# A routed feed-forward kernel: one product for the places of a tile's tokens, and transposes of gathered tokens on VectorE

## The chip, the core and the metric

The kernel runs on one core of one Trainium2 chip. The metric is device time in microseconds, from runs of the compiled program; less is better. All times below are in microseconds (us) unless marked ns. The engines are named as in the profile: PE is TensorE's matmul, PEld its weight load, DVE is VectorE, ACT is ScalarE, POOL is GpSimd, and SP is the queue that issues most DMAs.

## The reference

Tokens `x` are 64 sequences of 32, each of width 256 (2048 tokens). Three residual steps follow each other: cross-attention of 16 heads to a context of 257 rows of 128, self-attention of 4 heads with a rotary embedding, and a feed-forward layer with 8 experts, of which each token takes two. Cut to the part that the change touches:

```python
def _L0_ffn_ref(x, Wr, br, Wl1, bl1, Wl2, bl2, biases_N):
    D, H, N, K = (256, 512, 8, 2)
    scores_BSN = jnp.einsum('bsd,nd->bsn', x, Wr) + br
    w_BSN = jax.nn.softmax(scores_BSN, axis=-1)
    _, idx_BSK = jax.lax.top_k(scores_BSN + biases_N[None, None, :], K)
    val_BSK = jnp.take_along_axis(w_BSN, idx_BSK, axis=-1)
    val_BSK = val_BSK / jnp.sum(val_BSK, axis=-1, keepdims=True)
...
    h_NM2H = jnp.einsum('md,ndh->nmh', x_MD, Wl1) + bl1[:, None, :]
    a_NMH, b_NMH = (h_NM2H[..., :H], h_NM2H[..., H:])
    y_NMD = jnp.einsum('nmh,nhd->nmd', jax.nn.silu(a_NMH) * b_NMH, Wl2) + bl2[:, None, :]
...
    y_MD = jnp.einsum('mn,nmd->md', ew_MN, y_NMD)
...
x = x + _L0_ffn_ref(_layernorm(x, axis=-1), ...)
```

## The kernel before

Everything is float32. The work is cut into 16 tiles of 128 tokens (four sequences each), and has two stages with an overlap between them.

**The attention stage.** A loop over 64 sequences (L971) writes out PE's order by hand. For each sequence it transposes the probabilities (`probs_transposed`, L336), issues the scores of the next sequence (L313) and mixes the context (L346). Between these steps, `step()` advances three generators: "near" and "far", which are `rest` (L532) of the two tiles before, and "ahead", the next queries. `rest(t)` does the output of cross-attention, self-attention and the routing of tile t. PE and SP keep the order of the code (L79); the order on DVE, ACT and POOL is chosen by the compiler's scheduler from the same program.

**Routing** (`route`, L474) has three parts between two yields. It transposes the normalised tokens `xr`. It forms the scores, the two best experts, `two` (one row of 8 for each choice, 0 or 1), `both` (their sum) and the weights of the experts, which are put into the row beside the token (a row `RW` is 256 numbers, 8 weights and the token's number). Then it finds each token's place among those of its expert: PE adds two products into `pk`, `before` × `both` (tokens of this tile that come earlier, L514) and `ones` × `seen` (all of the tiles before, L515). `at` adds the start of the expert's region, `seen` takes in `both` (L518), and `slots` are the two row numbers in the DRAM buffer `routed`, to which POOL scatters the tile's rows with two indirect DMAs (L525).

**The experts.** The rows of an expert are worked on in blocks of 128. Six early blocks are chosen from the counts after tile 12 (`early_blocks`), while the last tiles are still under way; up to 33 late ones are planned after tile 15 (`late_blocks`), of which 28 run in this trace. `counted` (L547) broadcasts the counts by the product of `ones` and `seen`. A block goes through these steps:
- `gathered` (L612): SP reads the block's first row from a small table and issues one DMA of 128 rows of 1060 B from `routed` into `xg` (five buffers).
- `weights` (L618): SP loads the expert's weights, 1028 KB and 640 KB, into one of three lanes, only if the expert differs from that of the block before in the lane.
- `prepared` (L628): PE transposes the two halves of the tokens into PSUM (L633), ACT copies them to `bxT` (L635, two buffers), DVE forms the block's gate and target rows (L638 to L647).
- `first_half` and `second_half` (L649, L666): 16 products (L661) of 128x128x128 into `pa` and `pb`, then ACT's silu (L675) and DVE's `g` (L680).
- `combined` (L687): four products (L692) of 256 columns, DVE's bias and gate (L697, L698) into `y` (four buffers), and POOL's indirect DMA that adds the 128 rows of `y` to the output (L699).

`run` (L1077) sets the order of PE and SP for the late blocks: in block b, the gather of b + 3, `prepared(b + 1)`, `first_half(b)`, `combined(b - 1)` and a weight load of b + 2, `second_half(b)`, and the other weight load of b + 3. In the first late block `last_early` (L1107) stands in the place of `combined`; it finishes the last early block and issues both weight loads of late block 2, behind the gather of block 3.

The parts that the change touches, with the profile's line numbers:

Of the kernel before, what the change touches and what calls it, by code (L numbers as in the profile page):

```python
# [16 lines left out]
P = 128  # L17
# [33 lines left out]
def block_kernel(  # L51
# [422 lines left out]
    def route(t, xr):  # L474

        nc.gpsimd.tensor_copy(xr[:, RW - 1 : RW], token[:, t : t + 1])
        xT = wk.tile([P, 2, P], FP, tag="xrT", name=f"xrT{t}")
        transposed(xT, xr, 2, f"r{t}", t < NT - 2)
        yield
        pr = bank([NE], f"pr{t}")  # L480
        for k in range(2):
            nc.tensor.matmul(pr, xT[:, k, :], wr_sb[:, k, :], start=(k == 0), stop=(k == 1))
        sc = sm.tile([P, NE], FP, tag="rsc", name=f"rsc{t}")
        nc.vector.tensor_tensor(sc, pr, br_bc, ALU.add)
        sel = sm.tile([P, NE], FP, tag="rsel", name=f"rsel{t}")
        nc.vector.tensor_tensor(sel, sc, bn_bc, ALU.add)
        top = sm.tile([P, 8], FP, tag="rtop", name=f"rtop{t}")
        nc.vector.max(top, sel)
        idx = sm.tile([P, 8], U32, tag="ridx", name=f"ridx{t}")
        nc.vector.max_index(idx, top, sel)  # L490
        idf = sm.tile([P, 2, 1], FP, tag="ridf", name=f"ridf{t}")
        nc.vector.tensor_copy(idf[:, :, 0], idx[:, 0:2])

        two = sm.tile([P, 2, NE], FP, tag="rtwo", name=f"rtwo{t}")
        nc.vector.tensor_tensor(
            two, expert_id2, idf.to_broadcast([P, 2, NE]), ALU.is_equal
        )
        both = sm.tile([P, NE], FP, tag="rboth", name=f"rboth{t}")
        nc.vector.tensor_tensor(both, two[:, 0, :], two[:, 1, :], ALU.add)
        nmx = sm.tile([P, 1], FP, tag="rnmx", name=f"rnmx{t}")  # L500
        nc.vector.tensor_reduce(nmx, sc, AX.X, ALU.max, negate=True)
        ex = sm.tile([P, NE], FP, tag="rex", name=f"rex{t}")
        nc.scalar.activation(ex, sc, AF.Exp, bias=nmx)
        nc.vector.tensor_tensor(ex, ex, both, ALU.mult)
        tot = sm.tile([P, 1], FP, tag="rtot", name=f"rtot{t}")
        nc.vector.tensor_reduce(tot, ex, AX.X, ALU.add)
        inv = sm.tile([P, 1], FP, tag="rinv", name=f"rinv{t}")
        nc.vector.reciprocal(inv, tot)
        ew = xr[:, D : D + NE]
        nc.vector.tensor_scalar(ew, ex, inv, None, ALU.mult)  # L510
        yield

        pk = bank([NE], f"pk{t}")
        nc.tensor.matmul(pk, before, both, start=True, stop=False)  # L514
        nc.tensor.matmul(pk, ones, seen, start=False, stop=True)  # L515
        at = sm.tile([P, 1, NE], FP, tag="rat", name=f"rat{t}")
        nc.vector.tensor_tensor(at[:, 0, :], pk, region[:, 0, :], ALU.add)
        nc.vector.tensor_tensor(seen, seen, both, ALU.add)  # L518
        nc.vector.tensor_tensor(two, two, at.to_broadcast([P, 2, NE]), ALU.mult)
        slot = sm.tile([P, 2], FP, tag="rslot", name=f"rslot{t}")  # L520
        nc.vector.tensor_reduce(slot, two, AX.X, ALU.add)
        slots = sm.tile([P, 2], U32, tag="rslots", name=f"rslots{t}")
        nc.vector.tensor_copy(slots, slot)
        for k in range(2):
            nc.gpsimd.indirect_dma_start(  # L525
                out=routed[:, :],
                out_offset=bass.IndirectOffsetOnAxis(ap=slots[:, k : k + 1], axis=0),
                in_=xr,
                in_offset=None,
            )  # L530

    def rest(t, cT, lastT, ut):  # L532

# [10 lines left out]
    def small(shape, name, dt=FP):  # L544
        return tb.tile([P] + shape, dt, name=name)

    def counted(name):  # L547

        pc = bank([NE], f"pc_{name}")
        nc.tensor.matmul(pc, ones, seen, start=True, stop=True)  # L550
        count = small([1, NE], f"count_{name}")
        nc.vector.tensor_copy(count[:, 0, :], pc)
        return count
# [35 lines left out]
    def number(meta, k, b, most):  # L589
        return nc.values_load(  # L590
            meta[0:1, k, b : b + 1],
            engines=[SP],
            min_val=0,
            max_val=most,
            skip_runtime_bounds_check_because="formed from counts that bound it",
        )

    class Blocks:
# [1 line left out]

        def __init__(self, name, n, lane):
            self.name, self.n, self.lane = name, n, lane
            self.meta = small([3, n], f"meta_{name}", U32)
            self.mine = small([n, NE], f"mine_{name}")
            self.gate = small([n], f"gate_{name}")
            self.to = small([n], f"to_{name}", U32)
            self.valid = self.spare = None
            self.xgs, self.xTs, self.ps, self.gs, self.experts = {}, {}, {}, {}, {}  # L610

        def gathered(self, b):  # L612
            xg = xp.tile([P, RW], FP, tag="xg", bufs=5, name=f"xg_{self.name}{b}")
            at = number(self.meta, 0, b, NE * CAP - P)
            nc.sync.dma_start(out=xg, in_=routed[bass.ds(at, P), :])
            self.xgs[b] = xg

        def weights(self, b, layers, sure=False):  # L618
            if b not in self.experts:
# [7 lines left out]

        def prepared(self, b):  # L628

            xg = self.xgs.pop(b)  # L630
            pt = bank([2, P], f"pxT_{self.name}{b}")
            for k in range(2):
                nc.tensor.transpose(pt[:, k, :], xg[:, k * P : (k + 1) * P], ident)  # L633
            xT = xp.tile([P, 2, P], FP, tag="bxT", bufs=2, name=f"bxT_{self.name}{b}")
            nc.scalar.copy(xT, pt)  # L635
            self.xTs[b] = xT
            gates = xp.tile([P, NE], FP, tag="gates", name=f"gates_{self.name}{b}")
            nc.vector.tensor_tensor(gates, xg[:, D : D + NE], self.mine[:, b, :], ALU.mult)  # L638
            one = slice(b, b + 1)
            nc.vector.tensor_reduce(self.gate[:, one], gates, AX.X, ALU.add)  # L640
            if self.valid is None:
                nc.vector.tensor_copy(self.to[:, one], xg[:, RW - 1 : RW])
            else:
                nc.vector.scalar_tensor_tensor(
                    self.to[:, one], xg[:, RW - 1 : RW], self.valid[:, one],
                    self.spare[:, one], ALU.mult, ALU.add,
                )  # L647

# [7 lines left out]
        def of_half(self, b, half):  # L656
            w, _ = lanes[self.lane(b)]
            for j in range(4):
                for k in range(2):
                    lo = k * 2 * HID + (half * 4 + j) * P  # L660
                    nc.tensor.matmul(  # L661
                        self.ps[b][half][:, j, :], w[:, lo : lo + P], self.xTs[b][:, k, :],
                        start=(k == 0), stop=(k == 1),
                    )

# [41 lines left out]
    def early_blocks():  # L707


        bl = Blocks("early", EARLY, lambda b: b % 2)  # L710
        count = counted("early")
        full = in_blocks(count, 0, "early")
        last = up_to(full, "early")
        wide = [P, EARLY, NE]
# [20 lines left out]

    def late_blocks(done):

        bl = Blocks("late", LATE, lambda b: (b + 2) % LANES)
        count = counted("late")
        nb = in_blocks(count, P - 1, "late")  # L740
        nc.vector.tensor_tensor(nb, nb, done, ALU.subtract)

# [180 lines left out]

    before = iota([P], [[1, P]], 0, -1, "before")
    nc.vector.tensor_scalar(before, before, 0.0, None, ALU.is_gt)
    region = iota([1, NE], [[0, 1], [CAP, NE]], 0, 0, "region")
    expert_id2 = iota([2, NE], [[0, 2], [1, NE]], 0, 0, "expert_id2")

# [6 lines left out]

    early = iota([EARLY // 2, 2], [[1, EARLY // 2], [EARLY // 2, 2]], 0, 0, "early")
    early_expert = iota([EARLY, NE], [[0, EARLY], [1, NE]], 0, 0, "early_expert")
    row = iota([1], [[0, 1]], 0, 1, "row")
    minus_spare = iota([1], [[0, 1]], -TOK, -1, "minus_spare")
    token = iota([NT], [[P, NT]], 0, 1, "token")  # L940

    seen = const.tile([P, NE], FP, name="seen")
    nc.gpsimd.memset(seen, 0.0)
    none = xp.tile([P, RW], FP, tag="xg", bufs=5, name="none")
    nc.gpsimd.memset(none, 0.0)

# [129 lines left out]

    def run(lo, hi, before=None):  # L1077
        for b in range(lo, hi):
            if b + 3 < hi:
                blocks.gathered(b + 3)  # L1080
            if b + 1 < hi:
                blocks.prepared(b + 1)
            blocks.first_half(b)
            if b > lo:
                blocks.combined(b - 1)
                if b - 1 + LANES < hi:
                    blocks.weights(b - 1 + LANES, (1,))
            elif before:
                before()
            blocks.second_half(b)  # L1090
            if b + LANES < hi:
                blocks.weights(b + LANES, (0,))
            if b == 4:
                yield
        blocks.combined(hi - 1)
# [83 lines left out]
```

## Time and profile before

| what | value |
|---|---|
| median of 3 runs | 806.24 us (805.84 to 806.75) |
| the profiled execution's own time | 805.53 us |
| its span, first to last instruction | 803.8 us |
| PE busy | 774.1 us, 96% |
| DVE busy | 495.8 us, 62% |
| ACT busy | 377.9 us, 47% |
| POOL busy | 143.6 us, 18% |
| mean granted clock of TensorE | 0.995 |
| L633 pxT_late on PE | 56 matmuls, mean 275 ns |
| L635 bxT_late on ACT | 28 copies, mean 372 ns |
| L514 and L515 on PE | 32 and 32 matmuls, median 216 and 256 ns |
| L699 out_x<-y_late on POOL | 28 indirect DMAs, mean 1554 ns |

Matmuls are pipelined, and the profile gives each one the time until its result is there; the time that one takes from the next is the distance of their starts. The page's slices cut the span into 40 stretches of 20.1 us, each digit a busy share in tenths. In the timeline a row reads: start, duration, engine, line, operation, output<-inputs, shapes, count, and in brackets the engine's idle time before it and what ended it. A row with "x4" merges four instructions. Releasers are inferred from semaphores, and a wait for several of them is put down to the one that came last by the profile.

### The profile page before, as it was taken

To read this page: it belongs to the slowest core of one execution; us is meant where nothing else is said; L and a number is where in the kernel's file an instruction comes from. 1 tells how busy PE (TensorE), PEld (TensorE's weight loads), DVE (VectorE), ACT (ScalarE), POOL (GpSimd) and SP (SyncE) were. 2 spreads that over 40 slices of the span, in tenths; PEclk is the share of its full clock that TensorE was granted. 3 is DMA by queue.
4 is the path that set the end of the run, shared out by engine and by line. 5 is a ranking of instruction groups with operands and counts; after the bars stand their busy time and mean duration, and the time that the engine had idled before them with its cause. 6 is when DMAs were issued, how large, how long until landed. Compare 5 with 4: busy or idle time off the path is not lost. (4 is left out here: it accounts for less than half of the span.)

```text
span 803.8 us, 15150 instructions
## 1 busy us (share of the span) xinstructions
PE 774.1 (96%) x5212; PEld 609.9 (76%) x5212; DVE 495.8 (62%) x2045; ACT 377.9 (47%) x1078; POOL 143.6 (18%) x195
## 2 busy tenths in 40 slices
PE   8899999999999999999999999999998999999994
PEld 6576777777767777776777777766688899999994
DVE  5567666766775676668676667767655734334332
ACT  3565555556455555546455545654426322232230
POOL 3001011120211111020111111021133313332332
PEclk9999999999999999999999999999999999999998
DMA  9520202121020102012020202110531594356321
GB/s 308 165 89 1 66 11 67 28 73 60 18 80 12 67 10 87 12 69 73 18 67 11 67 11 67 40 47 15 192 136 34 138 400 124 54 150 207 54 42 22
DMA packets 32735, 64.14 MB, mean 80 GB/s; under 512 B 5328, under 2 KB 23632, under 8 KB 31120
## 3 DMA queue, kind: packets, MB, share of 16 engines
q1 hardware_dynamic: 26128, 54.08, 19.9%
q0 software_dynamic: 6528, 9.06, 6.2%
q8 instruction: 43, 0.70, 0.3%
q14 instruction: 36, 0.29, 0.1%
HBM read 87.54 MB, written 13.16 MB: 125 GB/s over the span
## 5 line engine op out<-in xcount | busy, mean ns | idle before, releaser
L318 ACT ACTIVATE pr<-s,nmx 128x257 f32<-128x257 f32 x256 | 121.7, 479 | 108.6 <-DVE nmx L317 100.4
L317 DVE TENSOR_REDUCE nmx<-s 128x1 f32<-128x257 f32 x256 | 105.9, 421 | 71.2 <-PE s L313 70.6
L313 PE MATMUL s<-kv,q 128*128 128x257 f32 x512 | 141.6, 385 | 1.5 <-ACT pr L318 1.4
L346 PE MATMUL pa<-pt,kv 128*128 128x512 f32 x256 | 123.2, 604 | 5.2 <-ACT ov L370 5.2
L313 PEld LDWEIGHTS s<-kv,q 128*128 128x128 f32 x512 | 88.2, 190 | 15.9 <-ACT pt L340 3.0
L325 DVE TENSOR_SCALAR pr<-pr,inv 128x256 f32<-128x256 f32 x256 | 82.0, 362 | 3.3
L336 PEld LDWEIGHTS tp<-ident,pr 128*128 128x128 f32 x512 | 61.1, 143 | 30.1 <-issue 15.5
L525 POOL DMA_INDIRECT routed<-xr,rslots x32 | 32.7, 1022 | 281.5 <-DVE lastT L1010 216.7
L336 PE MATMUL tp<-ident,pr 128*128 128x128 f32 x512 | 79.5, 277 | 1.6 <-DVE pr L325 1.6
L349 ACT COPY cT<-pa 128x512 f32<-128x512 f32 x64 | 37.5, 585 | 91.7 <-PE pa L346 91.7
L340 ACT COPY pt<-tp 128x512 f32<-128x512 f32 x128 | 75.4, 590 | 6.3 <-PE tp L336 6.0
L346 PEld LDWEIGHTS pa<-pt,kv 128*128 128x128 f32 x256 | 46.1, 190 | 39.6 <-issue 27.3
L699 POOL DMA_INDIRECT out_x<-y_late,to_late x28 | 43.5, 1554 | 107.4 <-DMA out_x<-y_late,to_late 36.0
L289 PE MATMUL pqh<-xqT,xwq_sb 128*128 128x256 f32 x256 | 60.8, 381 | 0.8 <-ACT xqT L196 0.8
L379 PE MATMUL po<-xwo_sb,ov 128*128 128x256 f32 x256 | 60.3, 379 | 0.0
L379 PEld LDWEIGHTS po<-xwo_sb,ov 128*128 128x128 f32 x256 | 48.6, 190 | 6.6
L289 PEld LDWEIGHTS pqh<-xqT,xwq_sb 128*128 128x128 f32 x256 | 47.3, 190 | 7.7 <-ACT xqT L196 1.3
L318 ACT ACTIVATION_READ_ACCUMULATOR pr<-s,nmx 128x1 f32 x256 | 51.8, 202 | 0.0
L323 DVE RECIPROCAL inv<-sums 128x2 f32<-128x2 f32 x128 | 20.6, 161 | 44.4 <-ACT pr L318 44.1
L635 ACT COPY bxT_late<-pxT_late 128x256 f32<-128x256 f32 x28 | 10.4, 372 | 73.2 <-PE pxT_late L633 73.2
L394 PE MATMUL pqkv<-awqkv_sb,xaT 128*128 128x512 f32 (+1 forms) x128 | 43.9, 486 | 0.0
L354 POOL TENSOR_TENSOR xb<-x,xbo_bc 128x256 f32<-128x256 f32 x16 | 11.6, 728 | 165.3 <-issue 116.6
(259 smaller groups left out, 1281.4 us busy)
## 6 DMA issues: line engine op xcount, KB each, us to landing
lane<-in_wall SPq DMA_DIRECT2D x24, 1028.0 KB
lane<-in_wall SPq DMA_DIRECT2D x24, 640.0 KB
lane2a<-in_wall SPq DMA_DIRECT2D x10, 1028.0 KB
kv<-in_ctx_t SPq DMA_DIRECT2D x16, 514.0 KB
kv<-in_ctx_a SPq DMA_DIRECT2D x16, 512.0 KB
lane2b<-in_wall SPq DMA_DIRECT2D x10, 640.0 KB
xg_late<-routed SPq DMA_DIRECT2D x28, 132.5 KB
x<-in_x SPq DMA_DIRECT2D x16, 128.0 KB
```

The source lines that it names most:

```text
L289: nc.tensor.matmul(pq[:, mm, :], xwq_sb[:, k, m * P : (m + 1) * P], xqT[:, k, :], start=(k == 0), stop=(k == 1),)
L313: nc.tensor.matmul(s, qb[:, g * P : (g + 1) * P], kvT[:, b, :], start=True, stop=True)
L317: nc.vector.tensor_reduce(nmx, s, AX.X, ALU.max, negate=True)
L318: nc.scalar.activation(pr[:, g, :], s, AF.Exp, bias=nmx, accum_out=sums[:, g : g + 1])
L325: nc.vector.tensor_scalar(pr[:, i, :ML], pr[:, i, :ML], inv[:, i : i + 1], None, ALU.mult)
L336: nc.tensor.transpose(tp[:, g * P : (g + 1) * P], pr[:, g, j * P : (j + 1) * P], ident)
L340: nc.scalar.copy(pt, tp)
L346: nc.tensor.matmul(pa, kvA[:, b, j, :], pts[j], start=(j == 0), stop=(j == MC - 1))
L349: nc.scalar.copy(cT[:, :, b, :], pa.rearrange("p (h n) -> p h n", n=SEQ))
L379: nc.tensor.matmul(po, ov[:, m, :], xwo_sb[:, m, :], start=False, stop=(m == XH // 2 - 1))
L394: nc.tensor.matmul(pq, xaT[:, k, :], awqkv_sb[:, k, lo:hi], start=(k == 0), stop=(k == 1))
L699: nc.gpsimd.indirect_dma_start(out=out[:, :], out_offset=bass.IndirectOffsetOnAxis(ap=self.to[:, b : b + 1], axis=0), in_=y, in_offset=Non ...
```

## The change

It has two parts and one small move.

First, the places of a tile's tokens. The kernel now keeps the running count in a tile `seen[t]` that is made from the product itself (`pk` + `both`), whose last row then holds the totals. POOL's `carry` keeps only this last row in `carried`. In tiles 0 to 13 DVE builds `fed`, which is `both` in all rows but the last and the totals in the last, and one product with `before_all` takes the place of two. Tiles 14 and 15 keep two products, the second with `of_last` and `seen` of the tile before. The early count takes the totals from `seen`; the late count adds a product of `ones` and the last tile's `both`, so that it needs no `seen` of tile 15.

Second, the transposes of the tokens of late blocks 3 and up. The gather lays the 128 rows out so that each 32x32 square of the transposed block lies on its own partitions: four DMAs of 128 pieces of 256 B and one of 128 pieces of 36 B (the weights and the number) into a tile `xw`. DVE then transposes all squares with one instruction straight into `bxT`. For this, position (p, k) of `bxT` holds column 2p + k of the token instead of 128k + p; the weights are laid out to match on the host. The early blocks and late blocks 0 to 2 keep the gather of one DMA and PE's transposes, now of every second column. L661 reads `bxT` in four runs of 32.

Third, `run` issues the gather of late block 3 behind the weight loads of late block 2.

```diff
         both = sm.tile([P, NE], FP, tag="rboth", name=f"rboth{t}")
         nc.vector.tensor_tensor(both, two[:, 0, :], two[:, 1, :], ALU.add)
+        boths[t] = both
+        if t < NT - 2:
+            fed = sm.tile([P, NE], FP, tag="rfed", name=f"rfed{t}")
+            nc.vector.scalar_tensor_tensor(fed, both, not_last, carried[t], ALU.mult, ALU.add)
...
         pk = bank([NE], f"pk{t}")
-        nc.tensor.matmul(pk, before, both, start=True, stop=False)
-        nc.tensor.matmul(pk, ones, seen, start=False, stop=True)
+        if t < NT - 2:
+            nc.tensor.matmul(pk, before_all, fed, start=True, stop=True)
+        else:
+            nc.tensor.matmul(pk, before, both, start=True, stop=False)
+            nc.tensor.matmul(pk, of_last, seen[t - 1], start=False, stop=True)
         at = sm.tile([P, 1, NE], FP, tag="rat", name=f"rat{t}")
         nc.vector.tensor_tensor(at[:, 0, :], pk, region[:, 0, :], ALU.add)
-        nc.vector.tensor_tensor(seen, seen, both, ALU.add)
...
+        if t < NT - 1:
+            seen[t] = sm.tile([P, NE], FP, tag="seen", name=f"seen{t}")
+            nc.vector.tensor_tensor(seen[t], pk, both, ALU.add)
+            carry(t)
+
+    def carry(t):
+        carried[t + 1] = sm.tile([P, NE], FP, tag="carried", name=f"carried{t + 1}")
+        nc.gpsimd.tensor_scalar(carried[t + 1], seen[t], is_last, None, ALU.mult)
...
-        nc.tensor.matmul(pc, ones, seen, start=True, stop=True)
+        nc.tensor.matmul(pc, of_last, seen[t], start=True, stop=more is None)
+        if more is not None:
+            nc.tensor.matmul(pc, ones, boths[more], start=False, stop=True)
...
         def gathered(self, b):
+            at = number(self.meta, 0, b, NE * CAP - P)
+            rows = routed[bass.ds(at, P), :]
             xg = xp.tile([P, RW], FP, tag="xg", bufs=5, name=f"xg_{self.name}{b}")
-            at = number(self.meta, 0, b, NE * CAP - P)
-            nc.sync.dma_start(out=xg, in_=routed[bass.ds(at, P), :])
-            self.xgs[b] = xg
+            if b < self.quarters:
+                nc.sync.dma_start(out=xg, in_=rows)
+                self.xgs[b] = xg, xg[:, D:]
+                return
+            xw = xp.tile([P, RW - D], FP, tag="xw", bufs=5, name=f"xw_{self.name}{b}")
+            for a in range(4):
+                nc.sync.dma_start(
+                    out=xg[a * SEQ : (a + 1) * SEQ, :D].rearrange("p (c e) -> p c e", c=4),
+                    in_=rows[:, a * 2 * SEQ : (a + 1) * 2 * SEQ].rearrange(
+                        "(c i) e -> i c e", i=SEQ
+                    ),
+                )
+            nc.sync.dma_start(out=xw, in_=rows[:, D:])
+            self.xgs[b] = xg, xw
...
-            for k in range(2):
-                nc.tensor.transpose(pt[:, k, :], xg[:, k * P : (k + 1) * P], ident)
-            xT = xp.tile([P, 2, P], FP, tag="bxT", bufs=2, name=f"bxT_{self.name}{b}")
-            nc.scalar.copy(xT, pt)
+            xT = xp.tile([P, 4, 2, SEQ], FP, tag="bxT", bufs=2, name=f"bxT_{self.name}{b}")
+            if b < self.quarters:
+                pt = bank([2, P], f"pxT_{self.name}{b}")
+                for k in range(2):
+                    nc.tensor.transpose(pt[:, k, :], xg[:, k:D:2], ident)
+                nc.scalar.copy(
+                    xT.rearrange("p c k i -> p k c i"), pt.rearrange("p k (c i) -> p k c i", c=4)
+                )
+            else:
+                nc.vector.transpose(
+                    xT, xg[:, :D].rearrange("p (c j k) -> p c k j", c=4, k=2)
+                )
...
-                        self.ps[b][half][:, j, :], w[:, lo : lo + P], self.xTs[b][:, k, :],
+                        self.ps[b][half][:, j, :].rearrange("p (c i) -> p c i", c=4),
+                        w[:, lo : lo + P],
+                        self.xTs[b][:, :, k, :],
...
+        bl = Blocks("early", EARLY, lambda b: b % 2, EARLY)
+        count = counted("early", max(seen))
...
+        bl = Blocks("late", LATE, lambda b: (b + 2) % LANES, 3)
+        count = counted("late", NT - 2, NT - 1)
...
+    of_last = const.tile([P, P], FP, name="of_last")
+    nc.vector.tensor_scalar(of_last, ones, is_last, None, ALU.mult)
+    before_all = const.tile([P, P], FP, name="before_all")
+    nc.vector.tensor_tensor(before_all, before, of_last, ALU.add)
...
     def run(lo, hi, before=None):
         for b in range(lo, hi):
-            if b + 3 < hi:
+            if b + 3 < hi and not (before and b == lo):
                 blocks.gathered(b + 3)
...
             elif before:
                 before()
+                blocks.gathered(b + 3)
```

## The prediction

> **What bounds the kernel now.** I read the slices first, then the timeline of the places that the diff touches, then the scatters' landings. The slices of the page:
>
> ```profile
> PE   8899999999999999999999999999998999999994
> POOL 3001011120211111020111111021133313332332
> PEclk9999999999999999999999999999999999999998
> DMA  9520202121020102012020202110531594356321
> ```
>
> PE is at nine tenths or more nearly everywhere, at the full clock, so an instruction taken from PE may pay. But POOL rises in the last quarter, the stage of the late blocks, and DMA is full in one slice there. A busy matmul record is no proof that PE is the limit, so the timeline of one late block comes next:
>
> ```profile
> 662.24 1.97 PEld L661 LDWEIGHTS pb_late<-bxT_late,lane 128*128 128x128 f32 x16
> 662.46 1.95 PE L661 MATMUL pb_late<-bxT_late,lane 128*128 128x128 f32 x16
> 664.24 0.38 PE L633 MATMUL pxT_late<-ident,xg_late 128*128 128x128 f32 x2
> 664.46 1.95 PE L661 MATMUL pa_late<-bxT_late,lane 128*128 128x128 f32 x16
> 669.76 0.38 PE L633 MATMUL pxT_late<-ident,xg_late 128*128 128x128 f32 x2
> ```
>
> The block repeats after 669.76 − 664.24 = 5.52 us, and PE issues without a hole: 34 instructions 0.11 apart and 8 of 256 columns 0.22 apart are 5.5. (Each float32 product is recorded as two matmuls: 448 records for 28 × 8 products.) The two transposes are "0.38" long in this view, yet the next matmul starts 0.22 after them. What goes with them is 0.22, not their duration.
>
> The other chain of this stage is POOL's. Its timeline, and the answer on the scatters' line:
>
> ```profile
> 670.00 1.55 POOL L699 DMA_INDIRECT out_x<-y_late,to_late  x1 [5.26 <-DMA out_x<-y_late,to_late]
> 674.58 1.55 POOL L699 DMA_INDIRECT out_x<-y_late,to_late  x1 [3.02 <-DVE y_late L698]
> 679.47 1.55 POOL L699 DMA_INDIRECT out_x<-y_late,to_late  x1 [3.34 <-issue]
> 684.04 1.59 POOL L699 DMA_INDIRECT out_x<-y_late,to_late  x1 [3.02 <-DMA out_x<-y_late,to_late]
> ...
> 764.03 1.55 POOL L699 DMA_INDIRECT out_x<-y_late,to_late  x1 [3.31 <-DMA out_x<-y_late,to_late]
> 768.64 1.55 POOL L699 DMA_INDIRECT out_x<-y_late,to_late  x1 [3.06 <-DVE y_late L698]
> 774.12 1.55 POOL L699 DMA_INDIRECT out_x<-y_late,to_late  x1 [3.92 <-DVE y_late L698]
> ...
> 790.45 1.55 POOL L699 DMA_INDIRECT out_x<-y_late,to_late  x1 [3.75 <-DVE y_late L698]
> 795.00 1.55 POOL L699 DMA_INDIRECT out_x<-y_late,to_late  x1 [3.00 <-DVEq L1121]
> DMA to landing us min/median/max: 3.6/3.9/8.9
> ```
>
> The engines named in the brackets were mostly long done. By the landings each scatter from 644 to 764 starts 0.75 us after the one before it has landed: scatter 3 lands at 678.73, scatter 4 starts at 679.47. It is a serial chain of some 4.5 to 4.9 us a scatter, longer where weights load (6.8 at 663, 5.6 to 6.7 at 717 to 736). The results wait for it: block 7's y begins at 684.73 and is scattered at 693.33, 8.6 late. The lag shrinks by about 0.8 a block since PE needs 5.52; at block 22 (y at 767.51, scatter at 768.64) it is gone, and only the last six scatters follow PE. **This is the point of the case: PE gives the pace of the late blocks with little to spare before the scatters do.** The last scatter starts at 795.00; the 8.75 to the span's end I leave as they are.
>
> **Part 1: one product for the places.** In the attention stage the sequence around the two products is the same in every tile:
>
> ```profile
> 194.80 0.28 PE L514 MATMUL pk<-rboth,before 128*128 128x8 f32 x2
> 194.94 0.37 PE L515 MATMUL pk<-seen,ones 128*128 128x8 f32 x2
> 195.17 0.64 PE L336 MATMUL tp<-ident,pr 128*128 128x128 f32 x4
> ```
>
> From the record starts, the second product opens at 194.94 and the transposes at 195.17: 0.22 us go with it. Fourteen tiles lose it. In tiles 0 to 11 PE issues at a constant rate around it (its one wait of a tile, 0.37 for ov L370, stands elsewhere and moves along): 12 × 0.22 = 2.7. The transposes right after it read pr; VectorE's last normalisation of it ends 0.37 before the last of them starts, while elsewhere 0.15 is the least distance, so 0.22 can just be had; in the other sequences shown it is 1.6 or more. Tile 12 gives nothing: its product is followed by the early count, for which PE waits 1.02 until VectorE's seen (551.70). The new seen is written in the code behind slots, three operations of about 0.17; between no loss and 0.5 I take a loss of 0.4. Tile 13 gives nothing either, as PE then waits for cT anyway (0.33).
>
> VectorE gains fed (nearest row: g_late's scalar_tensor_tensor is 344 ns for 128 columns, to_late's 214 for one; I take 0.2) in 14 tiles, 2.8 us of a busy 68 in 100, many microseconds ahead of the product. The new seen reads PSUM as rat does (160 ns against 158). POOL gains fifteen products of 128x8: between COPY's 180 and the 728 of 128x256 I take 600, by rstd's 128x1. In tile 15 rstd on POOL has PE waiting (1.41 at 618.10); a carry before it would cost up to 0.6, but POOL idles 1.49 just before and I put 0. In tile 15 seen falls away from VectorE's chain to the late gathers (0.1 at most); the late count gets one more product (0.22) behind a4, and I let them cancel. Four set-up operations on VectorE, 0.2 to 0.4 each, lie in the first 40 us where it is busy 22: between 0 and 1.5, I take 0.2.
> Sum of part 1: 2.7 − 0.4 − 0.2 = 2.1 earlier; bounds 1.2 and 2.8.
>
> **Part 2: the transposes.** 25 blocks × 0.22 = 5.5 us less PE. ACT loses 25 copies of 372 ns, none of which PE waits for here. VectorE gains a transpose of 128x256: its 128x32 takes 204 ns and 32x128 takes 302, so 1.02 ns a column and some 433 ns. It stands where gates stands now, behind g (ends 665.63 and 671.14), with VectorE then idle 2.28 until y; needed only by the next block's first half, 4 us later. If it stood ahead of g, py would lose some hundredths at most: it starts 0.62 after g is whole, 0.40 once PE is 0.22 quicker, against 0.43. Because the wait for a gather so moves from PE's queue to a place 5 us before the need, the later gathers, and gather 3 moved behind 1.67 MB of weights, cost PE nothing. What is queued behind the waiting transpose on VectorE is y and the next g; the tightest gather, block 4's, lands at 652.8 for 654.5, and the five issues of gather 3 that now come behind the weights (0.34 each on SP) take nothing that PE waits for. Blocks 0 to 2 and the early ones keep PE's transposes, now of every other column.
>
> The matmuls now read bxT in four runs of 32 columns. No row has that. From below it costs nothing; from above, four issues at the 28 ns that separate pk's 8-column matmuls are 112 against 110, 2 ns × 1088 = 2.2 us on PE. I take 0: the 64x32 matmuls of L424 issue 12 ns apart.
>
> The gathers: 5 DMAs instead of 1, 4 × 0.34 = 1.4 us more on SP a block, in a queue that issues three transfers in 5.5. By the packet records a median packet takes 48 ns for 1060 B, 18 for 256 B, 9 for 4 B, 27 for 512 B. Old: 128 × 48 / 16 = 0.38 us of all 16 engines. New: (512 × 18 + 128 × 10 + 64 × 9) / 16 = 0.69. So 0.3 more a block, from which PE is far and the scatters are not.
>
> The Trainium skill speaks against this (DMA: Bandwidth & Descriptors, Specifications): transfers under 512 B miss the line rate because they are read, modified and written. The trace agrees in direction, 14 B per ns at 256 B against 22 at 1060; if each small packet cost two of its recorded times, my estimate from that rule is 0.6 more a gather, and with it 0.3 an interval in the sum below, a loss of some 4 in this part.
>
> For the scatters: in 639 to 667 DMA is full (1.03) and a scatter takes up to 9.6; five gathers add 1.5 us of traffic, half of which the chain loses: 670.0 becomes 670.7. From there 19 intervals took 94.0; where a gather overlaps a scatter the interval is about 0.25 above the 4.5 of a free one, so I add 0.1 each: 1.9. The last six, once PE's wait is gone, are 4.7 + 5 × 4.55 (the last interval of the list) = 27.45. The last scatter starts at 670.7 + 94.0 + 1.9 + 27.45 = 794.05 instead of 795.0; PE's side would have it at 793.64 − 5.5 + 1.36 = 789.5. **Of 5.5 us on PE one arrives at the end.** Without any DMA cost it is 3.5; with 0.25 an interval and 1.2 at the start, a loss of 2.4.
>
> On the same subject the skill (TensorE: Matmul & The Clock Gate, Part 4: PE-mode transpose) gives about 275 ns for a transpose in a kernel. The records here say 273, but the issue distance is 110; 50 × 0.275 would be 13.8 off PE, where I count 5.5.
>
> **Sum.** The profiled execution took 805.53 (span 803.8). 805.53 − 2.1 − 1.0 = 802.4. It was 0.71 faster than the median of the runs, 806.24; on the median's scale the forecast is 803.1, −0.4%. Measurement can tell 0.2%, 1.6 us, from no change: 804.6 to 807.9.
>
> **Rivals.**
> Scatters bear the gathers for nothing, or keep up with PE: 806.24 − 2.1 − 3.5 = 800.6, or with 5.5, 798.6. For it: free intervals go down to 4.48. Against: 25 scatters from 670.0 to 789.5 would need 4.78 on average with the weights' three long ones, and they took 5.0.
> The first part is absorbed: fed or seen falls into VectorE's stretch right before the transposes of pr, whose margin is 0.22, so part 1 is 0 and 806.24 − 1.0 = 805.2: no change. For it: VectorE runs without a hole there (194.5 to 197.3). Against: the other sequences have 1.6 or more to spare.
> Slower: the small packets lengthen the serial scatters. Place: L699 from 670 to 768. If a gather's packets cost 27 ns, as the 512 B ones, that is 0.6 more a gather; taken in full by 19 scatters and half by five it is 12.9, less 2.1 + 3.5: 813.5. It decides from 0.26 an interval (5.6 / 21.5, the five counted half). For it: no slack in a serial chain. Against: the one row of 256 B says 18.
>
> **Chances.** Forecast (801.2 to 804.6) 0.45; free scatters 0.20; no change 0.21; slower 0.14. So faster by over 0.2% 0.65, within 0.21, slower 0.14. The range runs from 799.9 (2.8 and 3.5 off) to 807.8; it leaves out the slower rival and a quarter of the free one, 0.19.
>
> **What would show it.** A tile's L514 to L336 distance falls from 0.37 to 0.15, and tiles repeat 0.2 sooner. Late blocks repeat after 5.30, no L633 there but six records, a STREAM_TRANSPOSE of about 430 ns behind g. L699 stays 0.75 behind the landing to the end, and the last y waits some 5 us for its scatter. I am wrong if the last scatters follow y by 1.1, if PE waits for bxT, or if L661 issues wider than 0.11.

## The result, and the profile after

The changed kernel took 805.32 us (median, 801.64 to 810.31) where the kernel before took 808.13 (805.84 to 812.43) on the same chip: a ratio of 0.9972, 95% interval 0.9957 to 0.9988. That is 0.28% faster, 2.3 us, at the edge of what is told from no change. Forecast were 3.1 us, 806.24 to 803.1, with 801.2 to 804.6 as its band; 805.32 lies outside that band, beside a kernel before that now took 808.13. What follows shows that several terms of the forecast's sum were wrong.

The profiled execution took 805.14 (span 803.4; before 805.53 and 803.8). Because single executions of either kernel scatter over 5 us, I count by stretches. Starts are read from the timelines of PE's products: L313 opens a tile, L703 (before L661) `pa_late` opens a late block.

| stretch | before | after | difference |
|---|---|---|---|
| start to tile 1 | 47.35 | 48.17 | +0.82 |
| tile 1 to tile 15 | 499.01 | 497.80 | −1.21 |
| tile 15 to late block 0 | 90.48 | 91.15 | +0.67 |
| late blocks 0 to 27 | 148.81 | 148.08 | −0.73 |
| from there to the last instruction | 18.11 | 18.17 | +0.06 |

The first row can't be put down to the change: with the start-up code of before alone it runs from 47.3 to 50.2 over the profiles of the kernels below. So a single profile carries up to 3 us that belong to no edit, and what is said below rests on the other rows: together −1.21, inside the interval of the ratio (−1.0 to −3.5).

The slices of the page after, PE, POOL and DMA as before:

```profile
PE   8899999999999999999999999999998989999994
POOL 3001011220211111021111111121133312332332
DMA  9530202021020202022020202110531598448431
```

PE has a second slice of 8 where the late blocks begin, and DMA shows 9, 8, 4, 4 from there on, where before it showed 9, 4, 3, 5. The timeline of one late block, once the pace is regular:

```profile
721.60 1.95 PE L703 MATMUL pa_late<-bxT_late,lane2a 128*128 128x128 f32 x16
723.39 1.89 PE L736 MATMUL py_late<-lane,g_late 128*128 128x256 f32 x8
725.12 1.95 PE L703 MATMUL pb_late<-bxT_late,lane2a 128*128 128x128 f32 x16
726.90 1.95 PE L703 MATMUL pa_late<-bxT_late,lane 128*128 128x128 f32 x16
```

From 721.60 to 726.90 are 5.30, as forecast, and from `pa` to `py` 1.79 for 16 matmuls, so the four strided runs of the moving operand cost nothing (before, 653.42 to 655.21, also 1.79). VectorE's part of a block, from its timeline:

```profile
690.06 1.13 DVE L724 SCALAR_TENSOR_TENSOR g_late<-pb_late,lane,sa_late 128x128 f32<-128x128 f32 x4 [1.03 <-PE pb_late L703]
691.10 0.44 DVE L675 STREAM_TRANSPOSE bxT_late<-xg_late 128x256 f32<-128x256 f32 x1
```

The transpose takes 436 ns (median of 25; forecast 433), behind `g`. The attention stage, in the same sequence as in the prediction's fence:

```profile
195.47 0.28 PE L521 MATMUL pk<-rfed,before_all 128*128 128x8 f32 x2
195.60 0.67 PE L336 MATMUL tp<-ident,pr 128*128 128x128 f32 x4
```

From the product to the transposes it is 0.13 now instead of 0.37: PE was given its 0.22. The scatters' last steps, from POOL's timeline:

```profile
790.01 1.55 POOL L743 DMA_INDIRECT out_x<-y_late,to_late  x1 [3.43 <-DVE y_late L742]
794.61 1.55 POOL L743 DMA_INDIRECT out_x<-y_late,to_late  x1 [3.04 <-DVE y_late L742]
```

The last y begins at 793.19, so its scatter follows by 1.4 (before 1.4), where 5 had been forecast. The bound that I had called the point of the case did not end this execution. Where did PE's gain go? These are PE's waits from 636 to 690, late blocks 0 to 8:

```profile
PE pa_late L703 <- DMA lane<-in_wall: 1.6, 2, 1.2
PE pa_late L703 <- DVE gates_late L680: 0.8, 1, 0.8
PE pa_late L703 <- DMA lane2a<-in_wall: 0.7, 1, 0.7
```

(Columns: us in total, times, longest.) Before, no `pa_late` waited there at all. Distance n is the time from the first product of late block n to that of block n + 1. Distances 0 to 6 are 6.14, 5.37, 6.31, 6.76, 5.93, 6.19, 5.37: 42.1 in sum, against 38.7 before. These blocks lose 3.4, the twenty later distances gain 4.1; the difference is the −0.73 of the table. What delays the weights is on SP's queue. First the longest of its waits for a DMA in this window, then its timeline, and the same two weight loads in the kernel before:

```profile
SPq L643 <- DMA lane<-in_wall: 4.4, 4, 2.1
```

```profile
646.03 0.35 SPq L658 DMA_DIRECT2D lane2a<-in_wall  x1
647.53 4.01 SPq L643 DMA_DIRECT2D xg_late<-routed  x4
651.73 0.35 SPq L649 DMA_DIRECT2D xw_late<-routed  x1
652.50 0.35 SPq L658 DMA_DIRECT2D lane2b<-in_wall  x1
653.96 0.33 SPq L658 DMA_DIRECT2D lane<-in_wall  x1
```

```profile
646.51 0.34 SPq L624 DMA_DIRECT2D lane2b<-in_wall  x1
649.15 0.34 SPq L624 DMA_DIRECT2D lane<-in_wall  x1
```

The four pieces of one gather take 4.01 us to issue. In the trace SP's DMAs signal eight semaphores in turn, and each DMA waits until the one that used its semaphore before, eight issues back, has landed. With three issues a block eight of them reach back over two and a half blocks, and that wait was always over (before, SP waits for no DMA in this window). With seven they reach back about one block, to a weight load that is still on its way. The piece at 647.53 waited for a load that landed at 647.51, the next one for a load that landed at 650.17; it went out at 650.18, and the weights queued behind them at 652.50 and 653.96 instead of 646.51 and 649.15. DMA, busy without a gap from 640 to 667 before, is at 0.56 and 0.37 in 651 to 653.

### The profile page after: what moved, and what is told of

It is laid out like the page before. It is cut to its first block, busy times and chain, and to the rows that moved or that the text cites. A ratio compares the mean times of both kernels' runs of the same rounds, so it can differ in the third digit from the quotient of the medians.

```text
span 803.4 us, 15343 instructions
## 1 busy us (share of the span) xinstructions
PE 769.5 (96%) x5136; PEld 602.3 (75%) x5136; DVE 505.0 (63%) x2087; ACT 368.0 (46%) x1053; POOL 148.3 (18%) x211
## 5 line engine op out<-in xcount | busy, mean ns | idle before, releaser
L313 PE MATMUL s<-kv,q 128*128 128x257 f32 x512 | 141.6, 385 | 1.6 <-ACT pr L318 1.4
L313 PEld LDWEIGHTS s<-kv,q 128*128 128x128 f32 x512 | 88.5, 191 | 16.1 <-ACT pr L318 2.7
L325 DVE TENSOR_SCALAR pr<-pr,inv 128x256 f32<-128x256 f32 x256 | 80.1, 355 | 3.3
L719 ACT ACTIVATE sa_late<-pa_late,lane 128x128 f32<-128x128 f32 x72 | 20.5, 368 | 74.8 <-PE pa_late L703 70.7
L289 PEld LDWEIGHTS pqh<-xqT,xwq_sb 128*128 128x128 f32 x256 | 47.3, 190 | 7.7 <-ACT xqT L196 1.3
L546 POOL TENSOR_SCALAR carried<-seen,is_last 128x8 f32<-128x8 f32 x15 | 5.3, 353 | 218.7 <-DVE seen L541 218.7
```

Source lines behind the costliest of these rows:

```text
L289: nc.tensor.matmul(pq[:, mm, :], xwq_sb[:, k, m * P : (m + 1) * P], xqT[:, k, :], start=(k == 0), stop=(k == 1),)
L313: nc.tensor.matmul(s, qb[:, g * P : (g + 1) * P], kvT[:, b, :], start=True, stop=True)
L325: nc.vector.tensor_scalar(pr[:, i, :ML], pr[:, i, :ML], inv[:, i : i + 1], None, ALU.mult)
```

## The experiments

Two theories for the loss in the late stage at first: **SP**, the gathers' five issues hold back the weights through those waits; **C**, the scatters' serial chain is the limit by now. Distances and waits below are from one profile of each kernel.

**The parts alone.** `places_alone` is the kernel before with part 1, `transposes_alone` with part 2 and the moved gather.

> The kernel before with part 1 alone (one product for the places, carry, set-up; gathers and transposes as before). Theory of the prediction: 2.1 us faster, tile 15's first scores 2.5 us sooner than before, relative to the first tile's. Theory that the changed kernel's trace suggests (P): in odd tiles VectorE's rslot now stands ahead of the scores' maximum, ScalarE's exponentials start 0.1 us later after the product, and the values product (pov) waits for the PSUM buffer that ScalarE's copy of xqT frees; so only even tiles gain, 0.19 each: tile 15's first scores 1.0 us sooner than before, relative to the first tile's, and the time between 1 us faster and no change. Late blocks keep their distance of 5.52.

> The kernel before with part 2 and the moved gather alone (two products for the places as before). Theory of the prediction: PE waits for nothing among the late blocks, the last scatter is 1.0 us sooner. Theory S (each DMA issue of SP waits until the DMA eight issues before it has landed, so five more issues make gathers wait for weights, and the next weights stand behind them): PE waits about 4 us in all between late blocks 2 and 7, mostly for weights, and gains 0.22 a block from block 7 on, so that the last y is 1 us sooner; time 0.5 to 2 us under before. The first 40 us are as before if the 0.7 us of the changed kernel there come from the set-up operations.

Part 1 alone: ratio 0.9992 (0.9970 to 1.0014); tiles of 34.42 and 37.63 in turn, as in the changed kernel (before 34.58 and 37.64), but for two of 34.8; late distances 5.52 after the first two (5.75 and 5.59). Part 2 alone: 0.9993 (0.9976 to 1.0010); tiles as before, distances 5.53, 5.30, 6.32, 7.24, 6.01, 6.37, 5.37, then 5.30. So the late loss belongs to part 2, and the tiles' unequal gain to part 1. In this profile the last scatter starts 3.1 behind the last y, 1.7 more than usual: here the chain did hold the end. It is close by.

**Issues without data.**

```
 nc.sync.dma_start(out=xg, in_=routed[bass.ds(at, P), :])
+if self.name == "late" and b >= 3:
+  for i in range(4):
+    nc.sync.dma_start(out=xd[0:1, :], in_=routed[bass.ds(at, 1), D:])
```

> The kernel before, and behind each gather of late blocks 3 and up four DMAs of one row of 36 B into tiles that nothing reads: the same number of issues as the change, almost no bytes. Theory S: SP's gathers wait for weights' landing around 645 to 670, DMA falls under a half in between, PE waits 3 us or more in blocks 2 to 7 and keeps 5.52 afterwards; time 3 to 5 us over before. Theory D (the bytes of small packets are what delays weights): no difference over 1 us.

Ratio 1.0000 (0.9982 to 1.0017). SP's waits for landings appear, from a change that does nothing but issue:

```profile
SPq L615 <- DMA lane2a<-in_wall: 2.8, 2, 1.9
SPq L628 <- DMA lane<-in_wall: 1.9, 2, 1.6
```

But distances 0 to 6 sum to 40.04, only 1.4 over those of before. The mechanism is there, at half the price that I had expected.

**Small packets with one issue.** One more DMA a block that reads two 256 B pieces of each row.

> The kernel before, with one more DMA behind each late gather from block 3 on that reads two 256 B pieces of each row, 256 packets a block: about the traffic that the new gathers add (256 x 18 / 16 = 0.29 us a block), with one issue more instead of four. If traffic is what makes PE late in the weights' stretch, the distances of blocks 0 to 6 grow by 0.3 for each block, some 1.5 us in all, and SP does not wait; if it is the number of issues, they stay at 5.52 to 5.6. For the scatters: 0.1 to 0.3 more an interval from block 3 on, so the last scatter is 0 to 3 us behind where it was.

Ratio 1.0003 (0.9986 to 1.0020). No SP wait for a DMA; distances 6.08, 5.59, then 5.52: 0.6 over before, not 1.5. Nearly all of it is in distance 0, which runs from 5.52 to 6.91 over the profiles of this case without following the edits. The last scatter starts 1.4 behind y, as before. So this much traffic in small packets costs 0.6 at most. (The whole amount, four pieces of each row, has no time: its tiles do not fit into SBUF. `five_dmas_by_columns` below has as many small packets.)

**Away with the five issues, or with the chain.** The kernels with two outputs leave half of the late results out of the output; they serve to show the time without the chain.

```
-bl = Blocks("late", LATE, lambda b: (b + 2) % LANES, 3)
+bl = Blocks("late", LATE, lambda b: (b + 2) % LANES, 8)     # whole_gathers_...
```
```
+to_x = other if self.name == "late" and b % 2 else out      # ..._two_outputs
-    out=out[:, :],
+    out=to_x[:, :],
```

> The changed kernel, but late blocks 0 to 7 keep the one-DMA gather and PE's two transposes; the new gather and VectorE's transposes begin with block 8, when the weights' stretch is over. Theory SP (the five-DMA gathers delay the weights because SP waits for the landing of the DMA eight issues back): no SP wait for a DMA between 636 and 690, blocks 0 to 6 are 5.52 apart again (42.1 us in the changed kernel becomes 38.6), from block 8 on 5.30; the last y is 42.1 - 38.6 - 5 x 0.22 = 2.4 us earlier than in the changed kernel, counted from the second tile. Theory C (by now the scatters' serial chain is the limit): the last y is as early as that, but the last scatter follows it by 2 to 4 us instead of 1.4, and the end gains 0 to 1.5. If neither holds (the stalls come from the earlier pace of PE itself), the distances in blocks 0 to 6 stay above 5.52.

> The changed kernel, with the scatters of every second late block going to a second buffer in DRAM, so that two scatters need not follow one another; half of the late results are so left out of the output. It shows the end without the serial chain. Theory: since in the changed kernel the last scatter follows the last y by only 1.4, the end gains 0.3 at most; the lag of 9.4 in the middle shrinks to under 4. If the end gains over 1 us, the chain was still the limit there.

> Whole gathers up to block 7 and the scatters of every second late block to a second buffer (half of the late results left out of the output). Here neither the five-DMA gathers in the weights' stretch nor the chain can hold PE's gain back: the last y some 2.4 us earlier than in the changed kernel counted from the second tile, the last scatter 1.1 to 1.4 behind it, the end 2.4 earlier. The difference to whole gathers alone is what the serial chain takes: by theory C 1 to 3 us, by theory SP alone 0.

`two_outputs` (ratio to the kernel before 0.9992, 0.9967 to 1.0018): from late block 1 on scatters follow y by 1.1 to 1.2 (9.4 at most without the edit), yet from block 0 to the end it needs 164.37 against 166.25, of which 1.53 are shorter stalls in blocks 0 to 6. The chain's own share in the changed kernel is the other 0.35. Theory C falls as the cause of the loss.

`whole_gathers_to_block_7` (0.9984, 0.9966 to 1.0001): no SP wait for a DMA is left, as theory SP says, but distances 0 to 6 are 6.58, 7.03, 5.54, 5.53, 5.53, 5.53, 5.30: still 2.4 lost, in another place. PE's timeline there shows it waiting for a gather:

```profile
652.69 0.51 PE L670 MATMUL pxT_late<-ident,xg_late 128*128 128x128 f32 x2 [1.15 <-DMA xg_late<-routed]
```

With two outputs as well (0.9957, 0.9937 to 0.9977) it is 1.94 at the same transposes, in a distance of 7.81. (Distance 2 is 7.17 there with no wait in it: from 650 to 654 TensorE's granted clock was 0.68 and 0.50 in that profile.) Neither of my theories has the wait for the gather. What is left of the change in these blocks is the **moved gather**: in the trace of `whole_gathers_to_block_7` gather 3 is issued behind both weights of block 2, 5.0 after block 0's first product, and has landed at 12.9; before these were 1.2 and 7.2. That is theory M.

**The move alone, and taken back.**

```
-if b + 3 < hi:                                  # gather_moved_alone, on before
+if b + 3 < hi and not (before and b == lo):
     blocks.gathered(b + 3)
...
     before()
+    blocks.gathered(b + 3)
```

> The kernel before, with one edit: late gather 3 is issued behind the two weights of late block 2 instead of ahead of them. Theory M (the move itself costs PE a stall, since the gather then lands some 8 us later, about 652 instead of 644): PE waits for it ahead of block 3's transposes, 1.5 to 2.5 us in distances 1 or 2, and the blocks after it are 5.52 apart. Theory SP alone (only the number of issues matters): all distances 5.5.

> The changed kernel with late gather 3 issued where it was, ahead of the weights of late block 2; it still has five DMAs. Theory M: the 0.85 us that PE waits for VectorE's transpose of block 3 are gone. Theory SP: SP still waits for landings within 636 to 690 and blocks 3 to 6 still lose 2 to 3 us together against 5.30, since the five issues of each gather stand ahead of the weights as before. If both stalls go, the move was the whole cause and the waits of SP were only its effect.

The move alone costs one stall and nothing else, distance 1 being 8.04 and the others 5.5:

```profile
653.25 0.44 PE L633 MATMUL pxT_late<-ident,xg_late 128*128 128x128 f32 x2 [2.23 <-DMA xg_late<-routed]
```

Its last scatter follows PE, and the stretch from block 0 to the last instruction is 169.2 against 166.9. (Its ratio, 1.0005, 0.9985 to 1.0026, can't show 2.3 us.) `gather_not_moved` (0.9996, 0.9976 to 1.0016) has 6.77, 7.67, 5.37, 5.30, 5.58, 6.79, 5.37: the 0.85 of VectorE's transpose are gone, but 42.85 in sum, for SP waits 5.8 for weights now. Without distance 0 the sum is 36.1, and 36.0 in the changed kernel: to take back the move alone gains nothing. Theory M holds beside SP, not in its place.

**Both taken back**, with the one repair that part 1 suggests: `seen` written right behind `at`.

```
 at = ...
+if t < NT - 1:
+    seen[t] = ...; nc.vector.tensor_tensor(seen[t], pk, both, ALU.add); carry(t)
 nc.vector.tensor_tensor(two, two, at...)
```

> The changed kernel with three edits: one-DMA gathers and PE's transposes up to late block 7, gather 3 where it was, and the new seen written right behind at, ahead of slots. Late stage: distances 5.52 up to block 5 and 5.30 from block 6 or 7 on, no waits of SP for a DMA; from late block 0 to 27 some 144.4 us instead of 148.1 in the changed kernel and 148.8 before. Then by theory C the scatters are the limit again: the last one follows y by 3 to 5 us and the end gains about 0.5 to 1 on the changed kernel instead of 3.7. Attention stage: if the delay of VectorE's first nmx is what takes the 0.22 back in odd tiles, those fall from 37.63 to about 37.45 (7 x 0.2 = 1.3 us more) and even ones stay at 34.41; if not, they stay.

> One-DMA gathers up to block 7, gather 3 where it was, and the scatters of every second late block to a second buffer (half of the late results left out of the output). PE keeps all of its gain here: late block 0 to 27 in 144.4 us, last scatter 1.1 behind y, and the end 3.7 us ahead of the changed kernel counted from the start of the late blocks.

The second (0.9942, 0.9922 to 0.9963) has PE's whole gain: distances 5.53 or 5.54 up to 5, then 5.30, 144.51 from block 0 to 27 (before 148.81), last scatter 1.1 behind y, 162.3 from block 0 to the end. So with the gathers of five DMAs, and with them VectorE's transposes, out of blocks 3 to 7 and the move undone, nothing of the late loss is left. How the loss divides among them this run does not say. The first is the fastest of all: 801.88 (800.70 to 804.42) beside 808.12, **ratio 0.9927, 0.9900 to 0.9954**; the changed kernel had 0.9972, 0.9957 to 0.9988. Its distances are 6.91, 5.61, then the same as the other's, 145.96 in sum. The 1.4 of distance 0 is a wait for block 1's weights that comes and goes between profiles (0.6 in the changed kernel, nothing in `two_outputs`), and I have no cause for it. Its chain does not bind either: from block 23 on scatters follow y by 1.1 to 1.4. I had expected 3 to 5. Odd tiles fall to 37.51, even ones stay at 34.42; expected were 37.45.

**What else the five issues carry.** By then issues alone explained 1.4 of the 4.2 of `gather_not_moved`. Three more kernels.

```
+for i in range(4):                                          # five_dmas_by_rows
+    q = slice(i * 32, (i + 1) * 32)
+    nc.sync.dma_start(out=xg[q, :D], in_=rows[q, :D])
+nc.sync.dma_start(out=xg[:, D:], in_=rows[:, D:])
...
+    q = slice(i * 64, (i + 1) * 64)                         # five_dmas_by_columns
+    nc.sync.dma_start(out=xg[:, q], in_=rows[:, q])
```

> The kernel before, with each late gather from block 3 on in five DMAs as in the change, but cut by rows: four of 32 rows with 1024 B each and one of 128 times 36 B. Same order, PE's transposes as before, so neither the layout, nor the small packets, nor the faster pace of 5.30, nor the moved gather is in it. By small_packets_half (0.6 us lost) and four_tiny_dmas (1.4 lost) the count of issues alone would give 1.4 to 1.7 in distances 0 to 6; if the SP queue waits for each piece of real data that lands late behind weights, it is 3 to 4, nearly all that gather_not_moved lost (4.1 against 5.52). SP waits for landings of weights within 636 to 690 in both cases, some 3 to 6 us.

> The kernel before, with each late gather from block 3 on in five DMAs cut by columns: four of 128 pieces of 256 B and one of 128 times 36 B. Against five_dmas_by_rows (1.3 us lost in distances 0 to 6) it has the same number of issues and small packets as in the change; PE's transposes, pace and the gather's place are as before. If small packets together with five issues make up the rest of the change's loss, it loses 3 to 4; if the rest comes from PE's faster pace, about 1.3 again.

> gather_not_moved (the changed kernel with late gather 3 in its old place, five-DMA gathers from block 3 on), with two more transposes of a constant on PE for each of blocks 3 to 7, their result unread, so that PE's own pace there is 5.52 as before. If the loss of gather_not_moved (42.8 us for distances 0 to 6, against 38.6) comes from PE reaching the weights sooner, the sum stays 42.8 with shorter waits or falls a little; by five issues alone it would be 40.0. A sum of 41 to 42 would say that the five real gathers cost more than five by rows whatever the pace.

By rows: 1.0036 (1.0021 to 1.0050), by columns 1.0008 (0.9988 to 1.0028); distances 0 to 6 sum to 39.97 and 39.93, so both lose 1.3, whatever the packets' size; another 0.4 to 0.7 goes at the second group of weights, around block 17. At the old pace (0.9971, 0.9942 to 1.0000) the five gathers of the change still need 42.45, 4 us more than PE's own work: the pace isn't it. A hint, no more, are the weights' own packets: 8224 B took 330 ns on average before (636 to 668), 350 in the two five-DMA kernels, 370 and 379 in `gather_not_moved` and at the old pace; but 340 in the changed kernel itself, which lost as much. Nor is it VectorE: at the old pace each of its transposes ends 3.5 us or more before PE's product, and blocks 2 to 6 start 0.13 to 0.19 after their weights have landed. So some 2.7 us of what the crosswise gathers cost there beyond five issues by rows stay **open**.

## Why the prediction was near in size and wrong in its reasons

**"The later gathers, and gather 3 moved …, cost PE nothing": wrong, and the step that failed most.** Distances 0 to 6 were to be 37.3 (one of 5.52, six of 5.30) and were 42.1: a term put at nothing was 4.8. I had counted five issues of 0.34 on SP as time only; that an issue waits for a landing eight issues back couldn't be seen in a trace where this wait was always over, but the semaphores' numbers on SP's DMAs were there to be read. Alone, five issues cost 1.3 to 1.4. And I had the gather's need right but not its landing: the tightest gather was said to be block 4's, while gather 3, put behind 1.67 MB of weights, landed 5.7 later than before, counted from block 0's first product; with PE's transposes that is 2.2 past PE's need. With VectorE's transposes the landing is not what PE waits for. I had the transpose behind the `g` of the block before, some 4 us ahead of the need. For block 3 the scheduler put it a block later, between the first and the second instruction of block 2's `g`:

```profile
654.19 0.35 DVE L724 SCALAR_TENSOR_TENSOR g_late<-pb_late,lane,sa_late 128x128 f32<-128x128 f32 x1 [1.03 <-PE pb_late L703]
654.46 0.43 DVE L675 STREAM_TRANSPOSE bxT_late<-xg_late 128x256 f32<-128x256 f32 x1
```

The pieces of gather 3 had landed by 651.2, VectorE stood idle before 654.19 for PE's `pb`, and PE's 0.85 at 654.95 are this order. With the gather in its old place the transpose stands behind block 1's `g` and the stall is gone. Of the 4.8 in the changed kernel, then, 0.6 are distance 0, 1.0 is this order, and 3.1 are weights that landed late (blocks 4 to 6 start 0.13 to 0.14 after their landing). Five issues alone explain 1.3 to 1.4 of that; the cause of the rest stays open.

**"Of 5.5 us on PE one arrives at the end": near the −0.67 that came, by luck.** The pace (5.52 to 5.30), the transpose's length, its place but for block 3, and the free strided operand were as forecast. But the scatters were not what took the rest. The chain started earlier, not later: scatter 2 at 665.0 (before 670.0; forecast 670.7). That the gaps in the weights left DMA to it is likely, but not shown. Over all profiles with one output that start lies 28 to 34 us behind block 0, so my 0.7 had no standing beside this spread. The gathers' traffic was right (a gather's packets sum to 0.79 us of the 16 engines, against 0.48 before; forecast were 0.69 and 0.38), and the term of 0.1 an interval made of it is too small to see. So "free scatters" was right about the scatters and wrong about the time. With weights as before and no chain, blocks 0 to 27 gain 4.3 in `whole_gathers_not_moved_two_outputs`, though PE transposes for five more blocks there; with the chain they gain 2.9 in `whole_gathers_not_moved_seen_first`, where 1.4 went in distance 0. The rule that I weighed against the change (Trainium skill, DMA: Bandwidth & Descriptors, Specifications) is that transfers under 512 B miss the line rate because of a read-modify-write. It didn't decide: in `small_packets_half` a 256 B packet took 18 ns in the median and 18.7 in the mean among the weights (636 to 668), and all of that traffic cost 0.6 us at most.

**Part 1: 2.1 forecast, 0.5 came.** 1.21 were gained to tile 15, 0.67 lost behind it. The 0.22 arrives in each tile. Counted by the tile that is routed, most of it stays in the even ones (34.58 to 34.41), and nothing in the odd ones (37.64 to 37.63). There PE waits later, and the rival "absorbed" had the mechanism: VectorE runs without a hole there. Its order, relative to the product, is this in an odd tile before and after:

```profile
231.71 0.42 DVE L317 TENSOR_REDUCE nmx<-s 128x1 f32<-128x257 f32 x1
232.05 0.16 DVE L521 TENSOR_REDUCE rslot<-rtwo 128x2 f32<-128x16 f32 x1
```

```profile
232.22 0.17 DVE L529 TENSOR_REDUCE rslot<-rtwo 128x2 f32<-128x16 f32 x1
232.31 0.41 DVE L317 TENSOR_REDUCE nmx<-s 128x1 f32<-128x257 f32 x1
```

`rslot` slipped in ahead of the row maximum, which so starts 1.57 behind the product instead of 1.47. ACT's copy `qkT`, behind it, starts 2.54 behind the product instead of 2.46. The second half of PE's products `pov`, which waits for ACT's next copies, then starts at 4.84 in this tile, before at 4.80: PE's lead is gone. With `seen` first the maximum is at 1.44, the copy at 2.42, `pov` at 4.72, and odd tiles take 37.51: the order of three small operations was worth 0.12 in each of five tiles. In five of the nine profiles with part 1 one or two even tiles take 34.8 or so, in none without it; why is open.

Behind tile 15 the early count lost 0.3, near the forecast (0.4), against 0.22 that the tile's product had gained. Another 0.37 went at self-attention's scores, where PE waits more for ACT (waits from 546 to 637, after):

```profile
PE pc_early L566 <- DVE seen L541: 1.3, 1, 1.3
PE pss L424 <- ACT qkT L196: 0.7, 1, 0.7
PE pov L362 <- ACT cT L349: 0.6, 1, 0.6
```

Before these were 1.0, 0.5 and 0.3. But these 0.37 are not shown to be part 1's: four of the six other kernels without it lose 0.30 to 0.41 up to the same place, and `gather_not_moved_old_pace`, with it, loses nothing there. The late count's second product, which I had let cancel against a shorter chain on VectorE, cost its 0.22. So part 1's own gain is about 0.9: 1.21 less 0.08 and 0.22. The carry on POOL takes 0.31 in the tiles (600 ns were assumed) and delays no one.

**The rivals.** 805.32 is near what "absorbed" gave (805.2), but the kernel before had become slower too. That rival had part 1 at nothing and part 2 at 1.0; what came, by the profiles, was 0.5 and 0.7. The slower rival, small packets in the serial scatters, is refuted: the intervals from 670 to 770, without the weights' long ones (over 5.5), are 4.7 on average before and after.

## What to carry to other kernels

Before splitting a transfer, count the issues a loop turn on its queue and see from the trace's semaphores how far back each issue has to wait; a split that is free by its bytes can hold back the large transfer queued behind it. Move a gather only after reading when it lands behind its new predecessors, not when it is issued, and where the scheduler then puts what uses it. And where an engine runs without a hole, an instruction taken off another engine is kept only if the busy engine's order keeps its urgent operation first.

## What the runs showed of the hardware

- Each SP DMA waited for the landing of the one eight issues before it: no wait for a DMA between 636 and 690 before, 5.2 us after, 5.1 with four DMAs of 36 B a block.
- VectorE's transpose of 128x256 float32 takes 436 ns (25 times, 435 to 446).
- A matmul whose moving operand is read in four runs of 32 columns issues after 0.11 us like any other (1.79 for 16).
